# Softmax of a batch two turns behind its preparation instead of three, in the two causal attentions of a four-layer stack

## The chip, the cores and the metric

One core of a Trainium2 chip runs the whole program in a single launch. The metric is device time in microseconds (us), the median of three runs. The core has five engines that run side by side, each through its own list of instructions in a fixed order: PE (TensorE, matrix products; its weight loads are listed apart as PEld), DVE (VectorE), ACT (ScalarE), POOL (GpSimd) and SP (SyncE, which here only issues transfers). Transfers (DMA) are issued from SP, ACT and POOL and are carried out by 16 DMA engines. Engines wait for one another by semaphores; an engine whose next instruction must wait does nothing else meanwhile.

## The reference

The program is a stack of four layers on x with 8 sequences of 256 tokens and width 128 (2048 tokens), each layer a feed-forward block, an attention-like block, and the feed-forward block again. Two of the attention blocks are causal softmax attentions with 16 heads of 8 features, the one in layer 0 with 16 key heads, the one inside layer 3's block with 4 key heads that 4 query heads share each. What they compute, cut to its core:

```python
q, k = apply_rope(q, cos, sin), apply_rope(k, cos, sin)   # (batch, head, 256, 8)
s = jnp.einsum("bhqd,bhkd->bhqk", q, k) / np.float32(np.sqrt(8))
s = jnp.where(tril_mask, s, -jnp.inf)
att = jax.nn.softmax(s, axis=-1)
y = jnp.einsum("bhqk,bhkd->bhqd", att, v).transpose(0, 2, 1, 3).reshape(B, 256, 128)
x = x + y @ Wo
```

In layer 3 q and k are also normalised over their 8 features, and q has a gain. The softmax takes its maximum over the keys that a query sees; all of it is float32.

## The kernel before, in words

A batch is one sequence: 256 tokens, 16 heads. The class Chip does layer 0 on all 8 batches; layers 1 to 3 are done by two objects of the class Half, "a" and "b", each on 4 batches. Instructions of the two halves are woven together: while one half is in an attention, the experts of the other half's feed-forward block (lines 1600 and 1612 on PE) are meant to fill PE. So the attention code runs three times: once over 8 batches (l0_attn), and once over 4 batches in each half (l3_gqa).

Each batch goes through three pieces of work.

*Prepare* (prepare, put_values, attn_stack). The product qkv (line 738, or 1802 for all batches ahead of the loop in layer 3), the rotation of q and k (DVE and POOL, lines 746 to 751 or 1840 to 1845), a split of q and k into three bfloat16 parts each (split3), their transposes on PE (tpb, line 593), copies to sT, six transfers to DRAM (l_parts, line 600, three from SP and three from ACT, 192 KB each in layer 0), and two transfers back from SP (line 601) that stack the parts in 72 rows: qs (a tile of its own for each batch, four buffers) and ks (one of four fixed tiles, by b % 4). put_values copies v into one of four fixed tiles a["v"][b % 4] on POOL (line 567).

*Maxima* (attn_max). For each head the scores q·k with the mask added are made on PE (lines 617 to 619, tile sc), and DVE takes their maximum (line 621). In layer 0 two heads make one step, 8 steps a batch; in layer 3 one head, 16 steps. After the last step the negated maxima are put together (nm, lines 627 and 628), split in three (lines 573 to 576), transposed on PE (tpm, line 633), copied to mT, and sent on their way by two transfers from POOL: l_max to DRAM (line 637), and from there into rows 72 to 74 of qs (line 638). The second waits for the first.

*Mix* (attn_mix). The scores are made again, transposed (tile scT, lines 653 to 655), now over 75 rows, so that the maximum is already taken off in the product; ACT takes the exponential (line 658), PE multiplies with v (ctx, lines 668 and 670). A step is again two heads or one. After the last step ACT copies ctx (cs, line 673), PE sums (line 678), DVE takes the reciprocal (rec), POOL widens it (wide, line 682), PE brings it in place (shares, line 690), DVE multiplies (cT, line 692), PE applies the output weights (ao, line 700) and DVE adds to x (line 758 in layer 0).

attn_batches puts these in *turns*. Turn b prepares batch b, takes the maxima of batch b - 1, and mixes batch b - 3; the steps of maxima and mix take turns one by one, as the generators yield. With B batches there are B + 3 turns.

Two things set the order that the engines see. The code only names tiles; when the program is built, a planner puts the instructions of each engine in order by their place in the program and by when it expects their data. And tiles of one tag share a few buffers: sc and scT both carry tag "sc" with two buffers; in layer 0 the small products (tpb, tpm, sums, shares, ao, qkv) share tag "m" with three buffers, in layer 3 they share one. The lines in question:

```python
pss = ctx.enter_context(tc.tile_pool(name="l0asc", bufs=2, space=PSUM, reuse_waits="tile"))
sc = pss.tile([P, hp, 512], F32, name="sc", tag="sc")    # attn_max
sc = pss.tile([P, hp, 512], F32, name="scT", tag="sc")   # attn_mix
nc.gpsimd.dma_start(qs[72:75].rearrange("i h t -> i (h t)"), dr.rearrange("i h t -> i (h t)"))
```

The experts of the other half are tied to the attention's progress: self.step collects the last score product of each head, and an expert's products are ordered behind the step that stands at the same share of the stage (keep_pace, with 0.8 of it for half a's attention and all of it for half b's).

Of the kernel before, what the change touches and what calls it, by code (L numbers as in the profile page):

```python
# [165 lines left out]
class Chip:  # L166
# [538 lines left out]
    def attn_batches(self, a, prepare, finish, pool, psum, pss):  # L705

        qs = {}
        for b in range(self.B + 3):
            if b < self.B:
                q, k, v = prepare(b)  # L710
                self.put_values(a, b, v)
                qs[b] = self.attn_stack(a, b, q, k, pool, psum)
            steps = []
            if 1 <= b <= self.B:
                steps.append(self.attn_max(a, b - 1, qs[b - 1], pool, psum, pss))
            if b >= 3:
                steps.append(self.attn_mix(a, b - 3, qs.pop(b - 3), pool, psum, pss, finish))
            while steps:
                steps = [s for s in steps if next(s, s) is None]

# [1185 lines left out]
```

## Time and profile before

| what | us |
|---|---|
| median of the runs (lowest, highest) | 2827.74 (2826.46, 2832.05) |
| profiled execution, its own time | 2833.91 |
| span of the profiled execution | 2832.1 |
| PE busy, DVE busy, ACT busy, POOL busy in it | 2343.9, 1597.3, 1027.0, 319.1 |
| first attention: first qkv to last add to x | 238.2 to 493.2 |
| attention of half a in layer 3: first qkv to last ao | 2007.6 to 2173.4 |
| attention of half b in layer 3: first qkv to last ao | 2462.7 to 2634.7 |

A line of the profile reads: start in us, duration, engine, source line, operation, written tile <- read tiles, shapes, number of instructions merged into it, and in brackets the engine's idle time just before it with what ended it. A duration of several merged instructions goes from the start of the first to the end of the last. "128x768 f32" is partitions by elements. In a table by windows a row gives the window, its length, busy time of PE, PEld, DVE, ACT and POOL with the number of instructions, the clock that the throttle granted TensorE (1.00 is full speed), the busy share of the DMA engines and what they moved in GB/s. The profiled execution is one run; its times are compared with one another, and only their differences are carried to the median.

### The profile page before, as it was taken

The numbers are of one execution on the slowest core, as the hardware profiler recorded it, in microseconds if no ns is written. First come the engines' busy times: TensorE is split into PE (matmuls) and PEld (weight loads), VectorE is DVE, ScalarE is ACT, GpSimd is POOL, SyncE is SP. The second block draws the span as 40 slices with busy tenths as digits, with TensorE's granted clock in tenths as the row PEclk, the third lists the DMA queues.
The fourth block names the chain that finished last, engine by engine and source line by source line (L and its number), as shares of the span: only waits on it lengthen the run. The fifth ranks groups of instructions, "written<-read, shape, count | busy, mean of one in ns | idle before, by whom it ended". The sixth has DMA issues, their size and how long they took to land. (4 is left out here: it accounts for less than half of the span.)

```text
span 2832.1 us, 42755 instructions
## 1 busy us (share of the span) xinstructions
PE 2343.9 (83%) x17346; PEld 1554.8 (55%) x17346; DVE 1597.3 (56%) x3704; ACT 1027.0 (36%) x1754; POOL 319.1 (11%) x441
## 2 busy tenths in 40 slices
PE   5794788578789979868797898999698798779999
PEld 3672455367455445545465556666465565546666
DVE  6536442753558988778558745544654643453422
ACT  1121333211349578335453334312235321224322
POOL 0372110047000000000000000001201000210000
PEclk8695799779789999878998898999799899889989
DMA  7134331513200000110011001000211000030100
GB/s 258 21 42 108 103 86 49 195 24 41 81 15 17 16 29 17 31 30 24 7 40 31 17 16 50 1 16 17 68 47 37 27 8 16 26 93 3 43 23 23
DMA packets 103027, 127.27 MB, mean 45 GB/s; under 512 B 15161, under 2 KB 84094, under 8 KB 97726
## 3 DMA queue, kind: packets, MB, share of 16 engines
q1 hardware_dynamic: 61706, 71.56, 8.6%
q10 hardware_dynamic: 28836, 43.28, 4.6%
q0 software_dynamic: 12288, 9.71, 2.5%
q8 instruction: 136, 2.23, 0.3%
q14 instruction: 61, 0.50, 0.1%
HBM read 96.84 MB, written 27.53 MB: 44 GB/s over the span
## 5 line engine op out<-in xcount | busy, mean ns | idle before, releaser
L1612 PEld LDWEIGHTS po<-w_e,hT 128*128 128x128 f32 x2048 | 265.1, 198 | 69.4 <-issue 43.9
L1612 PE MATMUL po<-w_e,hT 128*128 128x128 f32 x2048 | 288.1, 286 | 11.8 <-DVE hT L1606 7.5
L1600 PE MATMUL ph<-x2T,w_e 128*128 128x512 f32 x512 | 266.0, 623 | 7.7 <-ACT hT L1608 7.1
L1608 ACT ACTIVATE hT<-ph,w_l_cols 128x512 f32<-128x512 f32 x192 | 131.4, 686 | 314.6 <-PE ph L1600 310.4
L621 DVE TENSOR_REDUCE nm<-sc 128x3 f32<-128x384 f32 (+1 forms) x192 | 130.3, 689 | 126.4 <-PE sc L619 125.4
L1040 PEld LDWEIGHTS po<-w_e,hT 128*128 128x128 f32 x1024 | 136.4, 199 | 80.7 <-DVE hT L1033 34.5
L658 ACT ACTIVATE pr_e<-scT 128x384 f32<-128x384 f32 (+1 forms) x192 | 111.3, 597 | 170.1 <-PE scT L655 163.4
L1040 PE MATMUL po<-w_e,hT 128*128 128x128 f32 x1024 | 146.2, 287 | 17.4 <-DVE hT L1033 13.3
L1030 PE MATMUL pu<-xnT,w_e 128*128 128x512 f32 x256 | 137.5, 620 | 8.8 <-ACT gs L1032 8.8
L231 PE MATMUL tp<-c_ident,xn 128*128 128x128 f32 x208 | 53.5, 377 | 104.3 <-DVE xn L251 96.3
L1027 PE MATMUL pg<-xnT,w_e 128*128 128x512 f32 x256 | 137.2, 618 | 1.8 <-ACT gs L1032 1.1
L1618 DVE SCALAR_TENSOR_TENSOR x_res<-po,gt,x_res 128x128 f32<-128x128 f32 x256 | 80.0, 357 | 90.0 <-PE po L1612 89.5
L500 ACT ACTIVATE gs<-pg 128x512 f32<-128x512 f32 x64 | 38.2, 597 | 247.4 <-PE pg L495 237.8
L1600 PEld LDWEIGHTS ph<-x2T,w_e 128*128 128x128 f32 x512 | 84.6, 195 | 70.7 <-ACT hT L1608 36.4
L1033 DVE SCALAR_TENSOR_TENSOR hT<-pu,w_l_bias,gs 128x512 f32<-128x512 f32 x128 | 94.7, 743 | 50.4 <-PE pu L1030 48.8
L1032 ACT ACTIVATE gs<-pg,w_l_bias 128x512 f32<-128x512 f32 x128 | 87.2, 688 | 87.7 <-PE pg L1027 79.9
L668 PE MATMUL ctx<-pr_e,vz 128*32 128x256 f32 x512 | 107.0, 397 | 2.8 <-ACT pr_e L658 2.7
L1758 DVE TENSOR_TENSOR gw<-sc,dec 128x768 f32<-128x768 f32 x64 | 61.2, 957 | 82.7 <-PE sc L1752 82.2
L513 POOL DMA_INDIRECT l_acc<-eo,idx x64 | 101.9, 1592 | 32.7 <-issue 16.8
L231 PEld LDWEIGHTS tp<-c_ident,xn 128*128 128x128 f32 x208 | 33.7, 169 | 124.8 <-DVE xn L251 81.3
L617 PE MATMUL sc<-ks,qs 72*128 72x256 bf16 x256 | 76.4, 298 | 25.2 <-DMA ks<-l_parts 14.1
L1046 ACT ACTIVATE ys<-po,pr 128x128 f32<-128x128 f32 x256 | 73.3, 368 | 64.4 <-PE po L1040 63.6
(604 smaller groups left out, 5000.0 us busy)
## 6 DMA issues: line engine op xcount, KB each, us to landing
l_parts<-sT SPq DMA_DIRECT2D x48, 192.0 KB, 5.2
qs<-l_parts SPq DMA_DIRECT2D x16, 576.0 KB
w_l_wu<-in_l_wu ACTq DMA_DIRECT2D x8, 1024.0 KB
w_e<-in_l_e SPq DMA_DIRECT2D x16, 512.0 KB, 3.6
w_e<-in_l_e ACTq DMA_DIRECT2D x16, 512.0 KB, 4.2
w_e<-in_l_e SPq DMA_DIRECT2D x16, 384.0 KB, 3.0
w_e<-in_l_e ACTq DMA_DIRECT2D x16, 384.0 KB, 3.0
l_parts<-sT ACTq DMA_DIRECT2D x24, 192.0 KB, 3.6
```

Of the source, the lines that this page charges most:

```text
L231: self.held(self.nc.tensor.transpose(ps[:, i * P : (i + 1) * P], src_of(g + i), self.ident), "tensor")
L513: nc.gpsimd.indirect_dma_start(out=accs[h][:, :], out_offset=bass.IndirectOffsetOnAxis(ap=idx[:, j : j + 1], axis=0), in_=eo[:, h, :], in_ ...
L621: nc.vector.tensor_reduce(blocks[:, hp * pr : hp * pr + hp, :], sc[:, :, 0:384].rearrange("p h (k t) -> p h k t", t=P), AX.X, ALU.max, neg ...
L658: nc.scalar.activation(pe, sc[:, :, 0:384], AF.Exp, scale=float(1.0 / np.sqrt(np.float32(8.0))))
L668: nc.tensor.matmul(o, z, pe[:, 0:S], start=(j == 0), stop=False)
L1027: mm = nc.tensor.matmul(pg, wg[:, c], xnT[:, cols], start=True, stop=True)
L1030: self.keep_pace(nc.tensor.matmul(pu, wu[:, c], xnT[:, cols], start=True, stop=True), part)
L1033: nc.vector.scalar_tensor_tensor(hT[:, k, :], pu, w["l1_bias"][:, 1, e, k : k + 1], gs, ALU.add, ALU.mult)
L1040: nc.tensor.matmul(po[:, i, :], hT[:, k, i * P : (i + 1) * P], wd[:, k * P : (k + 1) * P], start=(k == 0), stop=(k == 1),)
L1600: mm = nc.tensor.matmul(ps, we[:, k * P : (k + 1) * P], xnew[:, 512 * g : 512 * g + 512], start=True, stop=True)
L1608: nc.scalar.activation(hT[:, k, :], ps, AF.Relu, bias=bias)
L1612: nc.tensor.matmul(po[:, i, :], hT[:, k, i * P : (i + 1) * P], we[:, (4 + k) * P : (5 + k) * P], start=(k == 0), stop=(k == 3),)
```

## The change

A batch is mixed in turn b + 2 instead of b + 3, that is, in the turn right after the one that takes its maxima. There are B + 2 turns. prepare, attn_max, attn_mix, the tiles, their buffers and the transfers are the same, and so is the number of each. What moves is the place of each batch's mix in the program's order: it now stands one turn earlier against the prepares and maxima of later batches.

```diff
     def attn_batches(self, a, prepare, finish, pool, psum, pss):
 
         qs = {}
-        for b in range(self.B + 3):
+        for b in range(self.B + 2):
             if b < self.B:
                 q, k, v = prepare(b)
                 self.put_values(a, b, v)
...
             if 1 <= b <= self.B:
                 steps.append(self.attn_max(a, b - 1, qs[b - 1], pool, psum, pss))
-            if b >= 3:
-                steps.append(self.attn_mix(a, b - 3, qs.pop(b - 3), pool, psum, pss, finish))
+            if b >= 2:
+                steps.append(self.attn_mix(a, b - 2, qs.pop(b - 2), pool, psum, pss, finish))
             while steps:
                 steps = [s for s in steps if next(s, s) is None]
```

## The prediction

> **What bounds the kernel now.** I read the page first, then the busy time by windows, then the order of time of PE, POOL and DVE around the turns. The page says where the bound is over the whole program: PE busy 83% of the span, DVE 56%, no queue or DMA engine near full. An average decides nothing for three stretches (236 to 493, 2003 to 2173 and 2459 to 2635 us) of very different kinds, so I cut it by windows.
>
> ```profile
> span 2832.1 us, 42755 instructions
> ...
> PE 2343.9 (83%) x17346; PEld 1554.8 (55%) x17346; DVE 1597.3 (56%) x3704; ACT 1027.0 (36%) x1754; POOL 319.1 (11%) x441
> ```
>
> By windows, the columns being length, then busy PE, PEld, DVE, ACT, POOL, then granted clock, DMA share, GB/s:
>
> ```profile
> 236.00:495.00 259.00, 203.48 (x1628) 129.04 (x1627) 116.88 (x259) 85.22 (x160) 34.40 (x89) 0.83 0.31 82
> ...
> 2072.00:2105.00 33.00, 32.38 (x232) 18.55 (x232) 13.51 (x32) 12.99 (x27) 1.07 (x2) 1.00 0.20 52
> 2105.00:2140.00 35.00, 35.00 (x268) 21.39 (x268) 12.59 (x28) 13.11 (x30) 2.69 (x5) 1.00 0.01 3
> ```
>
> In the first attention PE is busy 203 of 259 us at a clock of 0.83: it waits, and the chain from engine to engine sets the time. In the last two PE is full from 2072 on: the experts of the other half fill it. So the first attention can gain or lose what a wait is worth, the last two only what PE idles.
>
> Which chain? At the start of turn 5, where max of batch 4 begins:
>
> ```profile
> 346.73 0.29 PE L633 MATMUL tpm<-ident_b,nms 128*48 128x128 bf16 x2
> 347.41 1.06 PE L678 MATMUL sums<-c_sums,cs 128*128 128x8 f32 x8 [0.39 <-ACT cs L673]
> 349.66 1.16 PE L690 MATMUL shares<-c_ident,wide 128*128 128x128 f32 x8 [1.19 <-POOL wide L682]
> 351.76 2.05 PE L700 MATMUL ao<-w_l_wo,cT 128*128 128x128 f32 x8 [0.94 <-DVE cT L692]
> 353.60 2.77 PE L738 MATMUL qkv<-w_l_qkv,xnT 128*128 128x384 f32 x4
> 356.16 0.42 PE L617 MATMUL sc<-ks,qs 72*128 72x256 bf16 x1
> ...
> 357.23 0.42 PE L653 MATMUL scT<-qs,ks 75*128 75x256 bf16 x1
> ```
>
> The reader is to see two things. The tiles of one tag come up in program order: tpm, sums, shares, ao, qkv; and scT of mix 2, whose data had been ready for 27 us (its L638 was issued at 327.54), stands behind sc of max 4. Both share the two buffers of tag sc, so max and mix alternate strictly. That is the lever of this change: a mix whose row of maxima is late holds up the next max too.
>
> How late is that row?
>
> ```profile
> 322.45 0.18 DVE L627 TENSOR_TENSOR nm<-nm 128x16 f32<-128x16 f32 x1
> ...
> 325.55 0.55 POOL L637 DMA_DIRECT2D l_max<-mT  x1 [25.85 <-DVE mT L221]
> 326.10 0.62 POOL L682 COPY wide<-rec 128x512 f32<-128x512 f32 x1
> 327.54 0.53 POOL L638 DMA_DIRECT2D qs<-l_max  x1 [0.82 <-DMA l_max<-mT]
> ...
> 345.46 0.18 DVE L627 TENSOR_TENSOR nm<-nm 128x16 f32<-128x16 f32 x1
> ...
> 347.91 0.55 POOL L637 DMA_DIRECT2D l_max<-mT  x1 [12.84 <-ACT mT L223]
> 349.00 0.60 POOL L682 COPY wide<-rec 128x512 f32<-128x512 f32 x1 [0.54 <-DVE rec L680]
> 352.79 0.53 POOL L638 DMA_DIRECT2D qs<-l_max  x1 [3.18 <-DMA l_max<-mT]
> ```
>
> nm is the end of a batch's maxima. The row goes out by L637 and comes back by L638, which waits on POOL for the first. First leg 1.99 us quiet (325.55 to 327.54), 4.88 us beside the large copies of a prepare (347.91 to 352.79). The landing of L638 has no row; I give it the quiet leg, 2.0. So nm to row, R, is 322.45 to 329.5 = 7.1 us quiet and 345.46 to 354.8 = 9.3 us loaded. Today R costs nothing: a whole turn lies between.
>
> **The change part by part.** It adds and removes no instruction. It removes one turn of each loop (11 to 10, 7 to 6, 7 to 6), and moves each mix one turn forward: its scores, exponentials, ctx, sums, wide on POOL, shares, ao and residual add. It issues no DMA, but tpb and the copies of a later prepare (SP, ACT) now stand behind the ao of a mix that comes earlier, and the wide copy shares POOL with L637 and L638. Queued behind the wait of mix's first score are all other scores of both kinds on PE, behind them DVE's reductions and ACT's exponentials, and by these the next nm. So R enters the loop: turn = R + (first score of mix to nm).
>
> That second term W: 323.91 to 345.46 = 21.6 in turn 4, with sums, shares, ao, qkv and tpb inside; 357.23 to 378.33 = 21.1 and 413.28 to 433.33 = 20.1 in turns 5 and 7, where all but tpb come ahead of it, as they will; 434.79 to 453.83 = 19.0 in turn 8 without a prepare. I take 20.6.
>
> First attention. Mix 0: L638 of batch 0 is issued at 282.46, so its first score is at 284.5, against 302.97 now. But PE's hole before 303 is not free: max 1 (272 to 286) now stands behind mix 0, and prepare 3 (qkv at 291.00) behind ao of mix 0. Turn 2 with cold clock took 19.5 in today's first pair (302.97 to 322.45), and 1.5 for tpb: nm 1 at 305.5 (now 288.2). Five turns of 7.1 + 20.6 = 27.7 give nm 6 at 444.0; turn 8 without a prepare 7.1 + 19.0 gives nm 7 at 470.1 (now 453.83). Today's mean turn is (453.83 - 322.45)/5 = 26.3, since quick ones (23) alternate with ones that wait (32 to 33). Then mix 7 alone: the row 8.2 later (453.83 to 460.01, plus 2.0), scores to cs 14.8 (first exponential 470.59, cs 484.78, 0.6 for the scores), cs to the last add 8.4 (484.78 to 493.20): 501.5, against 493.2. **+8.3 us**: the saved turn is paid for by R in seven waits.
>
> A prepare is not late: qkv to the end of its reads took 331.25 to about 351.5 (DMA share 0.63 in 348 to 352, 0.00 after), so it lies 29 after nm, and max needs it 34 after. L637 is issued 3 after the next nm, about 31, just past those reads; if it falls into them, R is 9.3: up to +2.2 in six turns, +13 more.
>
> Two rules bear on this. Row: in 346.73 to 356 no gap of PE exceeds 1.19 us, yet the granted clock in 352 to 356 was 0.50 and qkv took 2.77 instead of 1.45 us. The Trainium skill, "TensorE: Matmul & The Clock Gate", Part 1, says that the array falls to half its clock after an idle window of about 3.4 us. By the rule such short gaps keep the clock up, W would be turn 8's 19.0 and five turns 1.6 shorter each: 8.3 - 8.0 = +0.3. By the trace the waits are cold, 20.6 and +8.3. I go by the trace. Second, "DMA: Bandwidth & Descriptors", Anatomy of one DMA, puts about 2.0 us fixed on each transfer that GpSimd issues. The quiet leg fits; the loaded one does not. By the rule R is 7.1 always, by the row up to 9.3. I take 7.1 and keep the rest for the range.
>
> The last two. R there is 2098.91 to 2106.19 plus 2.0 = 9.3, and 2591.35 to 2597.18 plus 2.0 = 7.8. Four waits each (mix 0 to mix 3). sums, shares and ao fill 3.1 (0.95 + 1.11 + 1.06), tpb 1.6 in two, experts may fill the rest: between 0 idle and 4 x 5 = 20. The nearest rows are today's waits for ks there, 2.09 us at 2072.42 and 3.03 at 2529.86: the experts did not come in. So 2.0 to 2.5 per wait, some 8, less these waits, which go because turn 2 gets longer: +5 each, **+10 us**. Without any filling +17 each, with all filled -3 each.
>
> Sum +18.3. The profiled execution took 2833.9 (span 2832.1 and 1.8 around it), 6.2 above the median of the runs shown; a difference carries over: 2827.7 + 18.3 = 2846.
>
> **The rivals.** *Faster*: R is hidden. If max runs ahead of mix while the row travels, or the free buffers of qs, ks and v let every turn be as quick as turns 4 and 8 (23.0 and 20.5), then nm 7 comes at 305.5 + 5 x 23.0 + 20.5 = 441.0, and the end, by the same 31.4 after it, at 472.4: -20.8 there, -3 in each of the others: 2801, or up to 2822 if a part is hidden. One mechanism decides it: a score of max must pass one of mix. Against it speaks 357.23 behind 356.16 above, with mix ready; for it, that the order of a new program is planned anew. 17%.
>
> *No change*: W warm (19.0, +0.3) and the experts fill (-3 to +3 in each of the others): within 0.2%, 5.7 us, about what a measurement of this kernel can tell from no change. 13%.
>
> *Much slower*: R loaded in most turns (+13), and the experts fill little (+7 each): +35 to +45, 2863 to 2873. For it, the first leg of 6.17 us at 291.76 to 297.93, against it, the 31 against 29 above. 18%.
>
> That the change doesn't happen can be left out: the row dependency and the loop bound are both plain in the code.
>
> **How the numbers follow.** The wait per turn, as summed: 52%, +6 to +32. With the much slower case 70% for slower. The low end takes in part of the faster case (2818), the high end nearly all of the much slower one (2872): 18% is left out.
>
> **What would show it.** mix 0's first score near 284 instead of 303; nm 1 near 305; turns nearly even at 27 to 28 instead of 22 and 33; PE waiting for qs<-l_max ahead of scT (L653), which it never does now, or behind it; the last add of the first attention near 501. I am wrong if sc of a max runs between nm and the row by more than one step, if turns of 23 us remain, or if PE stays full across nm in the last two.

## The result, and the profile after

The changed kernel takes 2904.6 us (median of four runs, 2899.49 to 2907.7) against 2829.89 us (2826.46 to 2836.29) for the kernel before: ratio 1.0265, 95% interval [1.0245, 1.0285]. It is slower by 74.7 us. The forecast had the side right (+18.3 us) and the size wrong by a factor of four, outside its range.

The page of the changed kernel, first the span, then the engines:

```profile
span 2904.6 us, 42759 instructions
...
PE 2379.6 (82%) x17346; PEld 1562.7 (54%) x17346; DVE 1600.6 (55%) x3704; ACT 1035.8 (36%) x1758; POOL 319.2 (11%) x441
```

PE does the same 17346 products in 35.7 us more of busy time and has about as much more idle time (2904.6 - 2379.6 = 525.0 against 2832.1 - 2343.9 = 488.2, +36.8). So half of the loss is PE standing still, and half is PE being busy longer with the same products; in the first attention it is busy 225.81 us instead of 203.48, at a granted clock of 0.76 instead of 0.83. By windows, with the columns as before: the first attention, and then a stretch in the middle and three at the end of half a's attention in layer 3.

```profile
236.00:530.00 294.00, 225.81 (x1632) 142.79 (x1631) 119.16 (x262) 85.88 (x160) 34.78 (x89) 0.76 0.27 72
...
2099.00:2118.00 19.00, 19.00 (x144) 11.25 (x144) 6.58 (x12) 5.91 (x13) 0.00 (x0) 1.00 0.00 1
...
2175.00:2194.00 19.00, 16.22 (x121) 8.40 (x121) 12.80 (x40) 8.41 (x15) 4.87 (x4) 1.00 0.00 1
2194.00:2213.00 19.00, 15.12 (x85) 8.96 (x88) 4.05 (x11) 5.22 (x12) 1.72 (x3) 0.71 0.01 3
2213.00:2232.00 19.00, 15.88 (x115) 8.84 (x115) 1.32 (x3) 6.26 (x13) 0.62 (x1) 0.86 0.00 0
```

The first attention now ends at 528.6, not at 493.2, and its granted clock is 0.76 where it was 0.83. In layer 3 PE is still full in the middle of the stage, but its last 57 us hold waits, and the last 38 of them a lower clock too; before, PE was full up to 2165 of 2173:

```profile
2140.00:2165.00 25.00, 25.00 (x226) 15.33 (x226) 2.64 (x5) 11.88 (x28) 0.62 (x1) 1.00 0.00 1
```

The turns are even now, as forecast, but too long. The starts of nm (L627) in the first attention are 276.6, 307.7, 339.5, 371.9, 404.6, 437.0, 471.1 and 497.0: 31.1 to 34.1 us apart in the six turns that still have a prepare or follow one, 25.9 in the last. The forecast had 27.7 and 26.1. One such turn, in the order of time of DVE, of POOL and then of PE (products of the maxima and of ctx left out):

```profile
339.55 0.18 DVE L627 TENSOR_TENSOR nm<-nm 128x16 f32<-128x16 f32 x1
```

```profile
342.65 0.55 POOL L637 DMA_DIRECT2D l_max<-mT  x1 [21.98 <-DVE mT L221]
343.20 0.62 POOL L682 COPY wide<-rec 128x512 f32<-128x512 f32 x1
344.64 0.54 POOL L638 DMA_DIRECT2D qs<-l_max  x1 [0.81 <-DMA l_max<-mT]
```

```profile
341.10 0.29 PE L633 MATMUL tpm<-ident_b,nms 128*48 128x128 bf16 x2
341.58 1.06 PE L678 MATMUL sums<-c_sums,cs 128*128 128x8 f32 x8 [0.19 <-ACT cs L673]
343.88 1.16 PE L690 MATMUL shares<-c_ident,wide 128*128 128x128 f32 x8 [1.24 <-POOL wide L682]
345.89 2.08 PE L700 MATMUL ao<-w_l_wo,cT 128*128 128x128 f32 x8 [0.85 <-DVE cT L692]
347.75 2.77 PE L738 MATMUL qkv<-w_l_qkv,xnT 128*128 128x384 f32 x4
350.31 0.42 PE L653 MATMUL scT<-qs,ks 75*128 75x256 bf16 x1
353.04 0.39 PE L593 MATMUL tpb<-ident_b,sp 128*128 128x128 bf16 x2 [2.31 <-ACT sp L573]
353.23 0.31 PE L654 MATMUL scT<-qs,ks 75*128 75x128 bf16 x1
```

Three things are to be seen. The row is quick: its second leg is issued 5.1 us behind nm (339.55 to 344.64), and the trace of this kernel shows when it lands: 2.58 us later (2.5 to 2.7 for the eight rows of this stage), at 347.2. That is 7.7 behind nm, 0.6 more than the quiet R of the forecast. But the first scT starts at 350.31, 10.8 behind nm, and nothing is shown as having released it: PE simply had other things ahead of it in its list, ao and qkv, at half clock (0.50 granted from 346.0 to 350.5). And of that mix only one product gets through; then tpb stands in the list and waits 2.31 us for ACT's split. PE's waits over the stage say the same (line waited for: us in total, times, longest):

```profile
PE tpb L593 <- ACT sp L573: 23.3, 8, 4.2
...
PE shares L690 <- POOL wide L682: 9.7, 8, 1.3
PE ao L700 <- DVE cT L692: 7.2, 8, 0.9
```

Before, these were 15.6 in 5, 4.2 in 5 and 2.7 in 3. A wait of scT for qs<-l_max, which the forecast named as the sign, does not appear among this stage's waits: the row is hidden behind a longer chain that stands in front of the same scores. In layer 3 it appears once in each half, ahead of mix 0 (2.3 and 3.7 us).

### The profile page after: what moved, and what is told of

Its sections match the earlier page's. It is cut to its first block, busy times and chain, and to the rows that moved or that the text cites. A ratio compares the mean times of both kernels' runs of the same rounds, so it can differ in the third digit from the quotient of the medians.

```text
span 2904.6 us, 42759 instructions
## 1 busy us (share of the span) xinstructions
PE 2379.6 (82%) x17346; PEld 1562.7 (54%) x17346; DVE 1600.6 (55%) x3704; ACT 1035.8 (36%) x1758; POOL 319.2 (11%) x441
## 5 line engine op out<-in xcount | busy, mean ns | idle before, releaser
L1612 PEld LDWEIGHTS po<-w_e,hT 128*128 128x128 f32 x2048 | 257.6, 195 | 66.7 <-issue 42.0
L1612 PE MATMUL po<-w_e,hT 128*128 128x128 f32 x2048 | 278.4, 282 | 11.5 <-DVE hT L1606 7.2
L1040 PEld LDWEIGHTS po<-w_e,hT 128*128 128x128 f32 x1024 | 135.2, 197 | 79.2 <-DVE hT L1033 34.8
L1040 PE MATMUL po<-w_e,hT 128*128 128x128 f32 x1024 | 145.3, 286 | 17.4 <-DVE hT L1033 13.3
L500 ACT ACTIVATE gs<-pg 128x512 f32<-128x512 f32 x64 | 38.2, 597 | 248.5 <-PE pg L495 248.5
L668 PE MATMUL ctx<-pr_e,vz 128*32 128x256 f32 x512 | 122.5, 413 | 2.5 <-ACT pr_e L658 2.1
L1033 DVE SCALAR_TENSOR_TENSOR hT<-pu,w_l_bias,gs 128x512 f32<-128x512 f32 x128 | 94.8, 744 | 47.8 <-PE pu L1030 46.1
L617 PE MATMUL sc<-ks,qs 72*128 72x256 bf16 x256 | 76.7, 299 | 24.0 <-DVE nm L621 12.1
```

Source lines behind the costliest of these rows:

```text
L617: nc.tensor.matmul(sc[:, jj, 0:S], qs[0:72, h, 0:P], k, start=True, stop=False)
L668: nc.tensor.matmul(o, z, pe[:, 0:S], start=(j == 0), stop=False)
L1033: nc.vector.scalar_tensor_tensor(hT[:, k, :], pu, w["l1_bias"][:, 1, e, k : k + 1], gs, ALU.add, ALU.mult)
L1040: nc.tensor.matmul(po[:, i, :], hT[:, k, i * P : (i + 1) * P], wd[:, k * P : (k + 1) * P], start=(k == 0), stop=(k == 1),)
L1612: nc.tensor.matmul(po[:, i, :], hT[:, k, i * P : (i + 1) * P], we[:, (4 + k) * P : (5 + k) * P], start=(k == 0), stop=(k == 3),)
```

## The experiments

Stage times below run from the first qkv to the end of the last ao, from each profile (the first attention, then half a and half b in layer 3); "turn" is nm to nm; "first score" is nm to the first scT after the mix's pause. All totals are medians. The kernel before has 254.6, 165.9 and 172.0 us in the three stages, the changed one 289.1, 193.2 and 196.0.

**Which attention, and is it the row?** Four kernels: the distance of two in the first attention alone, or in layer 3 alone; and both distances with a mix that reads 72 rows instead of 75, so that its scores do not contain the maximum and do not wait for the row (the row is still made and sent).

```diff
+        lag = 2 if a["kv"] == 16 else 3          # e1; the other way round in e2
-        for b in range(self.B + 2):
+        for b in range(self.B + lag):
...
-                k, q = ks[0:75, h // rep, :], qs[:, h, :]
+                k, q = ks[0:72, h // rep, :], qs[0:72, h, :]      # e3 (two behind), e4 (three behind)
```

> Mix two turns behind in the first attention (layer 0) only, three in the other two. The changed kernel's trace puts the last add of the first attention 35 us later than before. If each attention pays for itself (theory: the row of maxima enters every turn of each loop), this run is 33 to 37 us slower than before. If what the first attention loses is caught up further on, it is less than 20.

> Mix two turns behind in the two attentions of layer 3 only. By the trace the stage of half a is 27 us longer and that of half b 24; some 5 us less to do later on. Theory: 35 to 43 us slower than before, and together with the run of layer 0 alone the whole 73 us. Rival, that the experts of the other half that were pulled into the waits pay it back: under 20.

> Two turns behind, but mix reads the 72 rows of scores alone, without the row of maxima: the softmax is taken without the maximum off (the row is still made, sent and brought back, and nobody reads it). Theory row: with no row to wait for, the loss is gone: 2800 to 2835 us, turns of the first attention 23 to 27 us. Rival order: what costs is that the next prepare (qkv, tpb) now stands behind the ao of a mix of the turn before, with or without the row: 2880 to 2905, turns still 30 to 33 us.

> Three turns behind, mix without the row of maxima as in the run with two. Both theories: the row is a turn early here, so nothing is waited for and nothing changes: 2822 to 2834 us. More than 6 us off would say that three rows of contraction or the order planned for them matter by themselves.

| kernel | us | ratio to before | stages |
|---|---|---|---|
| e1, first attention only | 2868.96 | 1.0156 [1.013, 1.0181] | 289.3, 167.7, 172.1 |
| e2, layer 3 only | 2874.59 | 1.0167 [1.0146, 1.0188] | 255.2, 193.5, 198.0 |
| e3, two behind, no row | 2821.8 | 0.9982 [0.9968, 0.9996] | 248.8, 166.5, 168.6 |
| e4, three behind, no row | 2826.7 | 0.999 [0.9977, 1.0003] | 252.4, 167.9, 171.7 |

Each half of the change loses by itself, and layer 3 loses as much as the first attention (46.1 and 40.5 us over the 2828.46 us of before in these runs); the forecast had them at +10 and +8.3. Both lie some 3 us past the ends of what was expected of them, and their sum is 87 us where the whole change costs 76 over the same 2828.46; that difference was not followed up. Without the row's dependency the whole loss is gone, and the turn that is saved is worth a little: some 5 us by the medians of e3 and e4, whose intervals overlap. In e3 the turns alternate again (22.4, 33.4, 22.9, 31.9, 24.0, 33.9, 20.5), where 23 to 27 were expected. So the loss comes through the row, and not through the order of prepare and ao as such.

**A leg less and a leg more.** If the row enters each turn, its length must show.

```diff
-        dr = self.tc.dram_tile([3, 16, S], BF16, name="l_max")
-        nc.gpsimd.dma_start(dr.rearrange("i h t -> (i h) t"), mT)
-        nc.gpsimd.dma_start(qs[72:75].rearrange("i h t -> i (h t)"), dr.rearrange("i h t -> i (h t)"))
+        for i in range(3):                                                     # e5: no DRAM leg
+            nc.gpsimd.dma_start(qs[72 + i : 73 + i], mT[16 * i : 16 * i + 16])
...
+        nc.gpsimd.dma_start(d2.rearrange(...), dr.rearrange(...))              # e6: one more, dr to d2 to qs
```

> Two behind as in the changed kernel; the row of maxima goes from SBUF to SBUF in three transfers (one for each bf16 term) instead of through DRAM, so one leg of about 2 us is gone. Theory A, that the row enters every turn (through the order of TensorE written ahead of the run, in which the mix's first scores stand behind the normalisation and the next projection): 7 turns of the first attention and 6 of the last two become 2 to 4 us shorter, and with the mix's scores beside the normalisation a little more; 2904 falls to 2855 to 2885, first row-to-row intervals to 26 to 30 us (32.7 in the changed kernel). Rival B, that the chain sums, reciprocal, wide, shares, cT, ao, projection sets the turn and the row lies in its slack: within 8 us of 2904.

> Two behind; the row makes one more leg (a second DRAM buffer), so it comes some 2 to 4 us later. Theory A: 13 turns by 2 to 4 us, 2925 to 2955, intervals of the first attention 34 to 37 us. Rival B (row in the slack of the normalisation, which ends about 4 us behind the row in the changed kernel): 2900 to 2915, intervals as before.

e5 took 2863.19 us, ratio 1.0135 [1.0109, 1.0162]; e6 2945.9 us, 1.0422 [1.0393, 1.0452]. That is 41 us less and 41 us more than the changed kernel: the length of the row counts, and the rival's "within 8 us" is out. Whether it counts by its landing or by the order that the planner writes for it, these two totals do not say, and the sizes are odd. In the first attention e5's first score comes 6.2 to 6.8 us behind nm in turns 3 to 6 and these turns are 27.2 to 29.1 us (stage 258.9); e6's comes 13.8 to 14.8 behind and the turns are 34.6 to 36.0 (stage 303.8). A leg of 2.0 us moves the first score, 10.9 in the mean of these turns in the changed kernel, by 4.4 or by 3.4. Where it stands, in e5's order of time (POOL, then PE, with products of the maxima left out; its lines past 637 are one lower):

```profile
338.06 1.49 POOL L637 DMA_DIRECT2D qs<-mT  x3 [17.01 <-DVE mT L221]
```

```profile
337.88 1.06 PE L677 MATMUL sums<-c_sums,cs 128*128 128x8 f32 x8 [0.43 <-ACT cs L672]
...
340.22 2.08 PE L689 MATMUL shares<-c_ident,wide 128*128 128x128 f32 x8 [0.37 <-POOL wide L681]
342.09 0.42 PE L652 MATMUL scT<-qs,ks 75*128 75x256 bf16 x1
```

Here scT follows shares directly, and ao and qkv come later: five score products of the mix stand between shares and ao in seven of e5's eight mixes, none in the changed kernel and none in e6. So with a shorter row the planner wrote another order of PE. That raised the question whether the order or the landing makes the 10.8 us of the changed kernel. One thing held in all three: turn less first score is 21.4 in the changed kernel (mean of the same four turns), 21.4 in e5 and 20.8 in e6, the W of the forecast within a microsecond.

**Maxima ahead, and separate buffers.**

```diff
             if b >= 2:
+                for _ in range(8 // a["hp"] if steps else 0):     # e7: half of the maxima's steps first
+                    next(steps[0])
...
-            sc = pss.tile([P, hp, 512], F32, name="scT", tag="sc")
+            sc = pss.tile([P, hp, 512], F32, name="scT", tag="scT")   # e8, e9; pools with bufs=1 instead of 2
```

> Two behind; in each turn the maxima take half of their steps before the mix is started, so the row of maxima is on its way while the second half of the mix runs. Theory A: the row is covered by about 10 us of scores and exponentials, the loss of the changed kernel (75 us) goes nearly whole, and the two-turn program has one turn less in each attention: 2800 to 2840. Rival B (chain of normalisation and projection behind each mix sets the turn): it stays in the turn, 2870 to 2905. Rival C (maxima and mix need to alternate so that VectorE's maximum and ScalarE's exponential run side by side): 2840 to 2880, intervals even at 28 to 31 us.

> Two behind; score tiles of the maxima and of the mix no longer share two buffers in turn, each kind has one buffer of its own, so maxima need not wait for the mix of the same turn and the reverse. If the strict alternation carries the row into the turn: the maxima run ahead of a late mix, intervals of 25 to 30 us and 2840 to 2885. If it does not, or if one buffer for each kind costs as much (the next scores wait for the reduction or the exponential of the tile before, about 1 us for each of 16 tiles): 2895 to 2930.

> The control of two tags: three behind as before, score tiles of maxima and of mix in one buffer each. It gives the cost of a single buffer by itself. If strict alternation on shared buffers carries the row into the turn, a large part of the 2909 of two tags at two behind is the price of the single buffer: three behind with two tags then takes 2860 to 2890, and two behind is only 20 to 50 slower than it (75 with shared buffers). If the sharing has nothing to do with it, three behind takes 2828 to 2845 and the difference stays at 65 to 80.

e7 took 2844.6 us, ratio 1.0076 [1.0047, 1.0105], stages 261.7, 172.9 and 175.6: with the row under half of a mix, 60 of the 75 us are back, 5 us past the end of what theory A allowed and at the near end of rival C's. What is left is spread over the stages (7.1, 7.0 and 3.6 us). C, that being out of step costs something, fits by its total alone: the even turns of 28 to 31 us that it expected are not there (23.3, 22.7, 36.0, 23.0, 35.8, 24.2 and 27.4). What the rest is was not taken apart. e8 (two behind) took 2909.48 us, 1.031 [1.0276, 1.0343], and its control e9 (three behind) 2876.66, 1.0192 [1.0167, 1.0217]. By the totals two behind costs only 33 us with separate buffers, as the expectation for sharing as the carrier said. By the stages it doesn't hold: the first attention goes from 253.5 to 289.1, +35.6, just as with shared buffers (+34.5), while layer 3, which the single buffer has already made slow (192.9 and 204.4 in e9), does not change (196.3 and 202.6). And in e8 the maxima still end together with the mix (nm of batch 2 at 340.0, the last exponential of mix 1 at 340.4), so the buffers did not set them free. Whether the strict alternation is needed for the loss stays undecided by these two.

**Filling PE's waits.** Products that nobody reads, placed behind the copy of the row, were to keep the clock up:

```diff
+        ps = psum.tile([P, 512], F32, name="warm", tag="m")
+        for _ in range(12):                                        # e10; 24 in e11
+            nc.tensor.matmul(ps[:, 0:S], a["ident_b"][0:48, :], mT, start=True, stop=True)
```

> Two behind, with 12 products of 128x256 that nobody reads on TensorE behind the copy of each row of maxima; the order of TensorE keeps the mix's first scores behind ao and the projection, as in the changed kernel. It asks what the slow clock after the waits is worth. If the clock carries the loss (in the changed kernel ao and projection take 4.8 us in a turn at half speed, scores and transposes behind them run slow as well): 2 to 4 us a turn saved against 1.3 to 2.6 for the products, 2870 to 2900. If the place of the scores carries it: nothing is saved and the products are paid, 2910 to 2940.

> Two behind, with 24 such products. With so many the written order of TensorE turns: some four of the mix's scores stand ahead of ao and the projection, though the row still goes through DRAM in two transfers and lands no earlier. If the order carries the loss: turns of 27.5 to 30 us in spite of the added work (32.7 in the changed kernel), 2860 to 2895. If the landing of the row on the chip carries it: the products are added, 2930 to 2965, and TensorE is seen waiting for the row ahead of the scores.

e10: 2907.88 us, 1.0289 [1.0262, 1.0317]; e11: 2927.65 us, 1.0353 [1.0335, 1.037]. Both lie between their two expectations. The first attention took 286.0 and 289.1 us with the added work inside, where the changed kernel took 289.1. The filler in it adds up to 13.0 and 27.8 us, so it saved about what it paid, and not for the same reason. In e10 the order of PE is that of the changed kernel (no score of a mix ahead of its ao). The first score comes later, 12.7 us behind nm in the mean of turns 3 to 6, but the rest of the turn is 18.6 us instead of 21.4; the stage's clock is 0.79 instead of 0.76, and tpb waits for sp 11.1 us instead of 23.3, and which of these two it is was not separated. In e11 the order changed as it did in e5, with four score products ahead of ao; the order written by hand (e13, below) gives 258.9 us, and with 27.8 of filler 286.7, near the 289.1 measured. What spoiled e11 as a test of the clock is to be seen in its windows (the filler runs from 345.35 to 349.3):

```profile
341.00:344.00 3.00, 2.10 (x22) 1.21 (x23) 1.85 (x5) 1.73 (x3) 0.00 (x0) 1.00 0.64 172
...
344.00:347.00 3.00, 2.63 (x29) 1.87 (x27) 0.63 (x3) 0.80 (x2) 0.56 (x1) 0.96 0.05 14
347.00:350.00 3.00, 3.00 (x15) 2.07 (x13) 0.00 (x0) 0.00 (x0) 0.53 (x1) 0.50 0.04 8
```

The clock fell to 0.50 while PE was busy 3.00 of 3 us.

**The order by hand.** This run tests the order in the first attention. The row is left as it is (two legs, DRAM); ao of the batch before and the next prepare with its qkv stand behind the first step of the mix in the program, and ao and qkv are tied behind it in PE's list, without a semaphore. e14 does the same with the one-leg row.

```diff
+            if pr == 0:
+                self.mixed = mm                  # the mix's first step
...
+                self.behind(mm, self.mixed)      # ao and qkv: order on PE only
...
+            steps = [s for s in steps if next(s, s) is None]
+            while late:
+                finish(*late.pop())              # ao of the mix before
+            if b < self.B:
+                q, k, v = prepare(b)
...
             while steps:
```

> Two behind, row through DRAM as in the changed kernel, but TensorE's order written by hand: ao of the batch before and the next batch's projection stand behind the mix's first scores. If the written place of the scores makes the 11 us: first scores 7 to 8 us behind the maxima, turns of the first attention 28 to 29.5 us (that time and 21), first attention 260 to 268 us (289), the whole 2850 to 2880. If the scores' place doesn't matter and the chain of normalisation, projection and preparation sets the turn: turns stay at 31.5 to 33, the whole 2895 to 2910.

> The same order by hand and the row from SBUF to SBUF in one leg. If with the order mended what is left is the row's landing: 1 to 2 us a turn less than with two legs, turns of 26.5 to 28, the whole 2840 to 2865. If the order alone mattered: as with two legs within 6 us.

e13 took 2879.18 us, ratio 1.0179 [1.0147, 1.0211]. Its first attention (stage 258.9 us) has turns of 27.0, 28.2, 27.8, 27.4, 29.3 and 26.3, about the 27.7 of the forecast. The order of POOL and of PE in one of its turns (nm at 332.32; lines past 655 are two or more higher):

```profile
334.52 0.56 POOL L637 DMA_DIRECT2D l_max<-mT  x1 [15.78 <-DVE mT L221]
...
337.20 0.53 POOL L638 DMA_DIRECT2D qs<-l_max  x1 [0.67 <-DMA l_max<-mT]
```

```profile
334.34 1.06 PE L680 MATMUL sums<-c_sums,cs 128*128 128x8 f32 x8 [0.43 <-ACT cs L675]
336.59 2.08 PE L692 MATMUL shares<-c_ident,wide 128*128 128x128 f32 x8 [1.19 <-POOL wide L684]
...
339.81 0.39 PE L653 MATMUL scT<-qs,ks 75*128 75x256 bf16 x1
...
340.86 1.91 PE L702 MATMUL ao<-w_l_wo,cT 128*128 128x128 f32 x8
342.56 1.68 PE L746 MATMUL qkv<-w_l_qkv,xnT 128*128 128x384 f32 x4
```

The row's second leg is issued 4.9 us behind nm (5.1 in the changed kernel), yet the first score stands 7.5 behind it instead of 10.8, and qkv takes 1.68 us instead of 2.77. With the 2.5 to 2.7 us that this leg took to land in the changed kernel, the row is there at 339.7 to 339.9 (an estimate), where the first score starts. Now PE does wait for the row itself in the stage (once for 5.5 us, ahead of mix 0):

```profile
PE scT L653 <- DMA qs<-l_max: 7.8, 5, 5.5
```

So in the first attention the written order carries 30.2 us (289.1 to 258.9). e14, 2864.04 us, 1.011 [1.007, 1.015], takes off 10 us more there (248.8), with turns of 24.7 to 27.3. That is as short as the stage of e3, in which nothing waits for a row (248.8 too). Read against e3, the row costs 40 us in this stage at a distance of two, 30 of them by the order and 10 by the way through DRAM, and the shorter distance gives back the 6 by which e3 lies under the 254.6 of before. In layer 3 neither helps: 190.3 and 201.4 in e13, 191.9 and 194.6 in e14.

**Candidates.**

```diff
+                for _ in range(4 // a["hp"] if steps else 0):      # e12: a quarter ahead, and the one-leg row
+                    next(steps[0])
```

> Two behind, maxima a quarter of their steps ahead of the mix, and the row from SBUF to SBUF without DRAM: both covers together, the best candidate at two behind. The row has two of eight steps of the mix (some 5 us) beside it and one leg less. If the row is all that two behind costs: 2812 to 2832, level with the kernel before. If being out of step costs by itself (half ahead took 2845): 2835 to 2850.

> Candidate: in the first attention two behind, maxima a quarter of their steps ahead, row in one leg (that stage took 252.2 us in the run of both covers, 254.6 in the kernel before); in layer 3 three behind as before. The stage's 2.4 us should be all: 2822 to 2830, ratio 0.998 to 1.001. If the one-leg row or the quarter cost something outside the stage: 2832 to 2840.

e12 took 2853.85 us, 1.0098 [1.0081, 1.0115], worse than forecast: its first attention, 252.2, is quicker than before, its layer 3, 183.6 and 192.8, is not. e15 keeps the first and leaves layer 3 three behind: 2822.02 us, ratio 0.9975 [0.9958, 0.9992], stages 248.5, 165.5 and 171.8. It is ahead of the kernel before by a quarter of a per cent, just clear of the noise and at the edge of what was expected; its first attention gives 6 us. Its first attention by windows:

```profile
236.00:488.00 252.00, 201.72 (x1628) 130.25 (x1627) 116.81 (x258) 84.50 (x160) 38.20 (x97) 0.83 0.30 82
```

The clock is back at the 0.83 of before.

## Why the prediction was right in direction and wrong in size

*Right.* The row's dependency costs more than the saved turn brings: e3 shows it, and e5 and e6 that the row's length counts. How it enters a turn was not as forecast. The first score of mix 0 was forecast at 284.5 and came at 285.8; nm 1 at 305.5, came at 307.7; the tail from nm 7 to the last add at 31.4, measured 31.6 (497.0 to 528.6). Turns became even. The first leg stayed near its quiet 1.99 us in the first attention, so a loaded row has no part in that stage's loss; in layer 3 it took 2.0 to 4.1 us. Two of the forecast's own signs spoke against it: in the first attention PE never waits for the row, and in the pause of half a that is taken apart below PE stays nearly full across nm, which was to mean that it is wrong. Even the rival "much slower" ended at +45.

*The term that failed in the first attention: R in "turn = R + W".* R was 7.1, nm to the landing of the row. The row landed 7.7 behind nm in the turn shown, for its second leg took 2.6 us and not 2.0, but the first score, where W begins, came 10.8 behind it (10.4 to 11.3 in turns 3 to 7). W was 20.6 and measured 21.4 in turns 3 to 6, 22.9 in turn 7. The mistake could have been seen in the trace of before. The W came from turns in which "all but tpb come ahead of it, as they will": sums, shares, ao and qkv stand between nm and the first score. From nm to the end of qkv they take 345.46 to 356.37 = 10.9 us in the lines that the prediction shows. If they are ahead of the score, R is the longer of 7.1 and 10.9, not 7.1: turn = 10.9 + 20.6 = 31.5 with the forecast's own W, and 32.3 with the measured 21.4; turns 3 to 6 were 32.3 in the mean. In the sum, the forecast's five turns of 27.7 were 32.7: 19 us more by the first term and 6 by W. With nm 1 coming 2 later, nm 7 is 27 later than forecast (497.0 instead of 470.1), and with the forecast's 8.3 that is the 35.4 us by which the last add moved. Taking 7.1 needed the scores to be ahead of ao and qkv; e13 wrote that order by hand and got turns of 26.3 to 29.3 around the forecast's 27.7, and the last ao ends at 498.8, where the forecast had the last add at 501.5.

Why the order matters only now: three behind, the scores that follow nm had their row a turn ago, and in every second turn the mix paused for about 3 us only, in the others for about 12 (exponentials of mix 0 end at 322.9 and go on at 325.9; those of mix 1 end at 345.8 and go on at 358.2). In the changed kernel the five pauses that have a prepare beside them are 13.8 to 15.1.

*The rule on the clock.* The forecast went by the trace (waits of 1.2 us with a clock of 0.50) against the idle window of the Trainium skill's "TensorE: Matmul & The Clock Gate", Part 1, and that was the right choice (W measured 21.4, not 19.0), but it counted no more slow clock than the turns of before had: the clock of the stage fell from 0.83 to 0.76. In e11 it fell with PE busy. How much of the loss is the clock by itself was not separated; e10 and e11 were to do it and didn't, though the shorter rest of e10's turns says that the clock, or tpb's wait, has a share.

*The term that failed in layer 3: "2.0 to 2.5 per wait", +5 for each half.* It was +27.3 and +24.1, beyond even the +17 that the forecast gave for no filling. The experts did fill: in half a PE is busy 10.43 of the 11 us from 2123.2 to 2134.2 between two mixes. But the first scT stands behind sums, shares, ao, tpb and the experts' products there, 13.5 us behind nm (2120.7 to 2134.2), while the row lands at 2130.8; over the six later mixes of the two halves the row lands 7.8 to 11.2 us behind nm, near the forecast's 9.3 and 7.8, and the first score comes 8.9 to 13.5 behind it. The mix's scores pause three times in each half for 9.6 to 13.5 us, where no pause was over 3.2 before.

And filling is borrowed. Half a's stage has the same 280 expert products in both kernels. Before, 68 of them start in its last 57 us, one as late as 2169.2 of 2173.4. In the changed kernel the first two pauses take 40 and 38, the last one starts at 2172.9, and the third pause and the last 57 us have none: there the windows above show PE at 16.2, 15.1 and 15.9 of 19 us, and the clock at 0.71 and 0.86 in the last two. Taking the records of the stage together, overlaps counted once, half a's +27.3 is 11.6 us of idle PE, 14.9 on the attention's same 808 products, 1.4 on eight other products and -0.6 on the experts. Half b's +24.1 has 12.1 on the experts, 300 products instead of 238, 9.4 on the attention's products and 2.6 of idle PE: there work of a later stage was pulled forward. That fits stages that add up to 86 us in a program that lost 75. So the wait that the forecast priced at 2 us of idle PE was filled, and the filling was paid for later. That the row is the cause in layer 3 too is shown by e3; that the experts' fixed number turns it into this loss fits the trace, but no run took them away or held them back, so it is not shown. e13 and e14 show only that the first attention's remedy is not one here (in e13's first such pause 18 expert products still stand between shares and the first score), and e7 that half a batch of cover brings all but 7.0 and 3.6 us back.

*What was not tried*: the mix two behind in layer 3 with experts held back for its last turns; and maxima wholly independent of the mix's buffers.

## What to carry to other kernels

In the first attention the dependency that was moved closer cost not its latency (7.7 us behind nm) but what stood ahead of its reader in the reader's own list (10.8): before summing, write down the order of the engine's list and take the longer of the two. When a loop's distance is cut, ask for each link what covers it now. Here cutting it paid only where the late link was made shorter and given work to hide behind (e15: one leg less, a quarter of the maxima ahead), and only in the first attention. Where other work fills a wait, count it: layer 3 fits the reading that such work is free only if there is more of it than waits, which no run here shows.

## What the runs showed of the hardware

- The granted clock fell to 0.50 in the middle of uninterrupted products: in e11 from 0.96 to 0.50 over a stretch with PE busy 3.00 of 3 us, a few us after a stretch with 2.10 of 3. It stayed at 0.50 for about 10 us (the windows of 3 us from 344 to 359 have 0.96, 0.50, 0.50, 0.50 and 0.83), though from 347 on PE was busy 2.88 and more of every 3 us.
- A row sent from SBUF to SBUF in three parts cost POOL 1.49 us to issue, and its reader started 4.0 us after the first issue began (338.06 to 342.09, with shares ahead of it on PE until then), an upper bound for the landing of all three.
- The first leg of the row, from its issue to that of the second, took 1.99 us in the turn shown (342.65 to 344.64), 2.0 to 2.7 us for all rows of the first attention but mix 0's (3.8), and up to 4.1 in layer 3; before, it was up to 6.17 in the first attention. The second leg, from DRAM into three rows of qs, landed 2.5 to 2.7 us after its issue in the first attention of the changed kernel.
